# Spreading an output projection over all steps of an attention loop, with transposes a step later and other shares for three engines' copies

## Chip, core and metric

The kernel runs on one core of one Trainium2 chip. The metric is the device time of one execution in microseconds (us). Before the change the median of three runs is 1230.23 us (1226.86 to 1231.26).

## What is computed

Four layers are added to a residual stream `x` of 32 sequences, 32 tokens and 512 features, all in fp32. The first three mix features with weights picked per sequence. The fourth is attention with a paged cache, and the change is in it:

```python
q = einsum('bsd,ed->bse', x, Wq)   # 32 heads of 128
k = einsum('bsd,ed->bse', x, Wk)   # 8 heads of 128
v = einsum('bsd,ed->bse', x, Wv)
q = rope(rmsnorm(q, q_norm_w)); k = rope(rmsnorm(k, k_norm_w))
k_all = concat([k_cache[block_table], k])   # 512 cached keys and 32 new ones per sequence
v_all = concat([v_cache[block_table], v])
scores = where(valid, q @ k_all * SCALE, -1e30)
o = softmax(scores) @ v_all
x = x + o.reshape(b, s, 32 * 128) @ Wo.T
```

## The kernel before

**Two parts.** The first part (to about 421 us) does the three small layers and projects queries, keys and values. Queries, keys and new values go to DRAM scratch (`q_d`, `k_d`, `v_d`), and so does the residual stream (`x_d`). The second part is one loop of 264 steps (`for n in range(N + LAG)`), one step for each unit (sequence `b`, key head `g`): 32 sequences of 8 heads, and 8 steps to drain. A unit has four query heads times 32 tokens, so 128 rows. Four units of one sequence make a quad `(b, q)`, q = 0 or 1. Four sequences make a tile `t` of 128 tokens; there are 8 tiles.

**One step**, in the order in which it is written:

1. `scores` (lines 734, 735): two matmuls, 288 and 256 columns, into the one PSUM tile `s_ps`. VectorE then adds the mask and takes the row minimum in one pass (line 743), which frees `s_ps` for the next step.
2. `exponentials` (line 752): ScalarE, in place.
3. In steps 0, 2, 4 and 6 `projected(NCH - 1, FILLS[n], 2)`: the last piece of the value projection for one of four tiles that the first part left over (`FILL`, line 309).
4. From step 4 on, `place` for the quad that has been scored: step `n` handles part `j` of four of all four units at once. VectorE transposes 32x32 blocks into `turned` (line 765), and four copies of 32 partitions bring it into `placed`. ScalarE does `on_act` of the four (line 773), the rest goes to GpSimd when q = 0 (line 775) and to VectorE when q = 1 (line 777). `on_act` is 2, and 3 for q = 1 at the last part.
5. `share` (line 846, `f_ps`): the output projection of tile `t`, one or more of its 32 heads h, each one matmul of 512 columns, accumulated in one PSUM tile. The list `SHARE` says how many heads in which step; `BEGIN` is the first step, 36, and a tile has 32 steps. The list before has 30 entries, of which four are 0 and six are 2. The steps at 30 and 31 have none. So with n counted modulo 32, steps 2, 3, 17, 21, 25 and 29 project nothing. After the last head VectorE adds the residual (line 855) and SyncE stores the rows.
6. `values` (line 801, `o_ps`): four matmuls with the cached values for the unit of 8 steps ago. Its first matmul in a quad needs all four parts of `placed`. With the quad's last unit come the new values (line 813) and `keep`: VectorE takes the reciprocal of the sums (`rden`, line 825), scales `o_ps` into `os` (line 827) and transposes it into `ot` (line 830), which the output projection reads as weights. `ot` has three buffers, `os` and the residual tile `x3` one each.

**Loads.** At the first step of a sequence SyncE's queue issues, in this order: the second half of its queries (waits for the scores that used the buffer), its new values `vn` (wait for the matmuls of the sequence before the last), eight register loads with page numbers, the next sequence's new keys, its 16 pages of keys (line 194, 128 KB each), a page table; then, at the fifth step, the first half of the next sequence's queries (line 224). GpSimd issues four gathers of cached values (line 242). The instructions of PE, VectorE, ScalarE, GpSimd and SyncE stand in the loop's own order (`manual_schedule`); each engine works through its list in that order.

Of the kernel before, what the change touches and what calls it, by code (L numbers as in the profile page):

```python
# [12 lines left out]
F32 = mybir.dt.float32  # L13
I32 = mybir.dt.int32
AF = mybir.ActivationFunctionType
ALU = mybir.AluOpType
# [4 lines left out]
P = 128  # L21
# [36 lines left out]
def cond_resid_kernel(  # L58
# [104 lines left out]
    def load_table(b: int):  # L163

        pages_of[b] = const.tile([1, NPP], I32, tag="pages", name=f"pages_{b}", bufs=4)
        at = B + b * NPP
        nc.sync.dma_start(out=pages_of[b], in_=pick[:, at : at + NPP])

    class Picked:
# [18 lines left out]
                )  # L188
            )

        def transfer(self):
            for n, out in enumerate(self.dsts):
                row = self.src[ds(self.rows[n], 1)].rearrange(self.shape)
                self.eng.dma_start(out=out, in_=row)  # L194
                if len(self.rows) < len(self.dsts):
                    self.name_next()
# [24 lines left out]
    def load_queries(b: int, q: int):  # L221

        qts[b, q] = qp.tile([P, HALF * S], F32, tag="qt", name=f"qt_{b}_{q}")
        nc.sync.dma_start(
            out=qts[b, q], in_=q_d[b][:, q * HALF * S : (q + 1) * HALF * S]
        )
# [53 lines left out]
    def accumulator(name: str, long: bool = False):  # L280
        taken.append(name)
        pool = ps_m if long or len(taken) % 3 else ps_n
        return pool.tile([P, HID], F32, tag="mm", name=name)
# [17 lines left out]
        ws[c] = wqps[c % 2].tile([P, KC, HID], F32, tag="wq", name=f"wq_{c}")  # L301
        eng.dma_start(out=ws[c], in_=w_qkv[c])

    def project(c: int, t: int):
        w = ws[c]
        ps = accumulator(f"qkv_{c}_{t}", c >= (HQ + HK) // REP)
        x3 = x3t(t)
        for k in range(KC):
            nc.tensor.matmul(  # L309
                ps,  # L310
                x3[:, k, :],
                w[:, k, :],
                start=(k == 0),
                stop=(k == KC - 1),
            )
        if c >= (HQ + HK) // REP:
            c0 = (c - (HQ + HK) // REP) * HID
            vs = vsp.tile([P, HID], F32, tag="vs", name=f"vs_{c}_{t}")
            copied = nc.scalar.copy(vs, ps)
            if (c, t) == (NCH - 1, 0):  # L320

                with tc.issue_after(copied.ins):
                    nc.scalar.activation(warm, eps_t, AF.Exp)
            nc.scalar.dma_start(out=v_d[t * P : (t + 1) * P, c0 : c0 + HID], in_=vs)
            return None
        return SimpleNamespace(
            c=c, t=t, i=0 if c < HQ // REP else 1, ps=ps.rearrange("p (h d) -> p h d", h=REP)
        )
# [59 lines left out]
    def projected(c: int, t: int, lag: int):  # L388
        u = project(c, t)
        if u is not None:  # L390
            for stage in (squares, sums, roots, inverses, rotate, scales):
                stage(u)
            ready.append(u)
        if len(ready) > lag or (u is None and ready):
            store_heads(ready.pop(0))
# [364 lines left out]
    def place(b: int, q: int, j: int):  # L760
        if j == 0:
            placed[b, q] = tp.tile([P, QUAD, L // P, P], F32, tag="placed", name=f"placed_{b}_{q}")
        pr = prs[b, q][:, :, :L].rearrange("p u (c j s) -> p j u c s", j=P // S, s=S)[:, j]
        part = tp.tile([P, QUAD, L // P, S], F32, tag="turned", name=f"turned_{b}_{q}_{j}")
        nc.vector.transpose(part, pr)  # L765

        on_act = 3 if q == 1 and j == QUAD - 1 else 2
        for i in range(P // S):
            dst = placed[b, q][j * S : (j + 1) * S, :, :, i * S : (i + 1) * S]
            src = part[i * S : (i + 1) * S]  # L770
            dst, src = (a.rearrange("p u c s -> p (u c) s") for a in (dst, src))
            if i < on_act:
                nc.scalar.copy(dst, src)  # L773
            elif q == 0:
                nc.gpsimd.tensor_copy(dst, src)  # L775
            else:
                nc.vector.tensor_copy(dst, src)  # L777
# [14 lines left out]
    def values(b: int, g: int):  # L792
# [15 lines left out]
        if u == QUAD - 1:  # L808
# [5 lines left out]
            placed.pop((b, q)), prs.pop((b, q))  # L814
            keep(b, q)

    def keep(b: int, q: int):


        po = pos.pop((b, q))  # L820
        t, j = divmod(b, BT)
        if (t, q) not in ots:
            ots[t, q] = bp.tile([P, HALF, P], F32, tag="ot", name=f"ot_{t}_{q}")
        rden = tp.tile([P, QUAD], F32, tag="rden", name=f"rden_{b}_{q}")
        nc.vector.reciprocal(rden, dens.pop((b, q)))
        o = tp.tile([P, QUAD, D], F32, tag="os", name=f"os_{b}_{q}", bufs=1)
        nc.vector.tensor_tensor(  # L827
            o, po[:, :, :P], rden.unsqueeze(2).to_broadcast([P, QUAD, D]), ALU.mult
        )
        nc.vector.transpose(  # L830
            ots[t, q][:, :, j * S : (j + 1) * S],
            o.rearrange("p u (k d) -> p (u k) d", d=S),
        )

    pfs, x3s = {}, {}

    def load_residual(t: int):
        x3s[t] = tp.tile([P, HID], F32, tag="x3", name=f"x3_{t}", bufs=1)
        nc.sync.dma_start(out=x3s[t], in_=x_d[t])

    def finish(t: int, hs):

        for h in hs:
            if h == 0:
                pfs[t] = ps_p.tile([P, HID], F32, tag="f", name=f"f_ps_{t}")
            nc.tensor.matmul(  # L846
                pfs[t],
                ots[t, h // HALF][:, h % HALF, :],
                wo[:, h, :],
                start=(h == 0),  # L850
                stop=(h == HQ - 1),
            )
            if h == HQ - 1:
                x3 = x3s.pop(t)
                nc.vector.tensor_tensor(x3, x3, pfs.pop(t), ALU.add)
                nc.sync.dma_start(out=out[t * P : (t + 1) * P, :], in_=x3)

    LAG = 8

    SHARE = [1, 2, 1, 2] * 2 + [1, 2, 1] + [1, 1, 0, 1] * 4 + [1, 1, 2]
    BEGIN = BT * HK + LAG - QUAD

    def share(n: int):
        t, i = divmod(n - BEGIN, BT * HK)
        if 0 <= t < NT - 1 and i < len(SHARE):
            done = sum(SHARE[:i])
            finish(t, range(done, done + SHARE[i]))

    units = [(b, g) for b in range(B) for g in range(HK)]
    N = len(units)

    FILLS = {0: NT - 4, 2: NT - 3, 4: NT - 2, 6: NT - 1}
    order = {
        mybir.EngineType.PE,
        mybir.EngineType.DVE,
# [4 lines left out]
    with tc.manual_schedule(engines=order):  # L882
        for n in range(N + LAG):
            b, g = divmod(n, HK)
            if n == max(FILLS) + 1:
                pa.close()
                bp = ctx.enter_context(tc.tile_pool(name="b_w", bufs=3))
                ps_o = ctx.enter_context(tc.tile_pool(name="b_o", bufs=1, space=PSUM))
            if BEGIN <= n < N + QUAD and (n - BEGIN) % (BT * HK) == len(SHARE) - 2:

                load_residual((n - BEGIN) // (BT * HK))
            if n < N:
                if g == 0 and b >= 1:
                    load_queries(b, 1)
                    load_new_values(b)
                if g == 0 and 1 <= b < B - 1:
                    load_keys(b + 1)
                    keys = Picked(nc.sync, k_cache, pages_of.pop(b + 1), page_keys(b + 1), K_SHAPE)
                    load_new_keys(b + 1)
                    keys.transfer()  # L900
                    if b + 2 < B:
                        load_table(b + 2)
                if g == 0 and b >= 2:
                    load_values(b)
                if g == QUAD and b < B - 1:
                    load_queries(b + 1, 0)
                scored = scores(b, g)
                exponentials(*scored)
            if n in FILLS:

                projected(NCH - 1, FILLS[n], 2)
            if QUAD <= n < N + QUAD:
                bq, i = divmod(n - QUAD, HK)
                q, j = divmod(i, QUAD)
                if j == 0:
                    gather_new(bq, q)
                if j == 3:
                    flip_new(bq, q)
                place(bq, q, j)
            share(n)  # L920
            if n >= LAG:
                values(*units[n - LAG])
            if n < N and g == HK - 1 and b < B - 1:
                see_keys(b + 1)
            if n >= N + QUAD:
                at = 3 * (n - N - QUAD)
                finish(NT - 1, range(at, at + 3))
        assert not dens and not prs and not pos and not placed and not pns
        load_residual(NT - 1)
        finish(NT - 1, range(3 * QUAD, HQ))  # L930


# [74 lines left out]
```

## Time and profile before

| what | value |
|---|---|
| median of three runs | 1230.23 us |
| the profiled execution, its own time | 1226.37 us |
| its span, first to last instruction | 1224.6 us |
| granted TensorE clock | 0.999 |
| PE busy | 1183.7 us, 97% |
| VectorE (DVE) busy | 797.4 us, 65% |
| ScalarE (ACT) busy | 750.4 us, 61% |
| GpSimd (POOL) busy | 419.1 us, 34% |
| first scores of the loop start at | 421.55 us |
| scores of step 36 (first output projection) start at | 520.39 us |
| scores of step 132, 164 and 196 start at | 807.21, 902.82 and 998.78 us |
| scores of the last step with scores (255) start at | 1175.68 us |

A line of the timeline has the start in us, the duration in us, the engine, the kernel's line, the operation, what it writes and reads, and how many instructions are merged; in brackets stands the idle time before it and who ended it. A line of the waits has the waiting engine and line, the releaser, and then total us, times and the longest. One fp32 matmul of the kernel is two PE instructions, so "x2" is one matmul.

### The profile page before, as it was taken

The numbers are of one execution on the slowest core, as the hardware profiler recorded it, in microseconds if no ns is written. First come the engines' busy times: TensorE is split into PE (matmuls) and PEld (weight loads), VectorE is DVE, ScalarE is ACT, GpSimd is POOL, SyncE is SP. The second block draws the span as 40 slices with busy tenths as digits, with TensorE's granted clock in tenths as the row PEclk, the third lists the DMA queues.
The fourth block names the chain that finished last, engine by engine and source line by source line (L and its number), as shares of the span: only waits on it lengthen the run. The fifth ranks groups of instructions, "written<-read, shape, count | busy, mean of one in ns | idle before, by whom it ended". The sixth has DMA issues, their size and how long they took to land.

```text
span 1224.6 us, 19658 instructions
## 1 busy us (share of the span) xinstructions
PE 1183.7 (97%) x5480; PEld 749.1 (61%) x5480; DVE 797.4 (65%) x1787; ACT 750.4 (61%) x1657; POOL 419.1 (34%) x555
## 2 busy tenths in 40 slices
PE   8999999999999988899999999999999999999998
PEld 5444444444444456767767767767767777777764
DVE  3433597777774058866766777777767866876860
ACT  1233376565664268767767767867776776776760
POOL 2301443333332014434433433443334343433410
PEclk9999999999999999999999999999999999999999
DMA  8986756667655626766775676766666775776610
GB/s 323 420 333 254 261 144 153 168 178 198 160 124 161 213 84 219 234 217 194 226 228 188 219 230 201 229 199 220 220 210 196 243 224 173 247 227 188 215 57 9
DMA packets 180478, 250.63 MB, mean 205 GB/s; under 512 B 20978, under 2 KB 140146, under 8 KB 174610
## 3 DMA queue, kind: packets, MB, share of 16 engines
q1 hardware_dynamic: 157410, 165.35, 44.0%
q0 software_dynamic: 19216, 69.35, 16.7%
q10 hardware_dynamic: 3744, 14.68, 3.4%
q8 instruction: 44, 0.72, 0.2%
q14 instruction: 64, 0.52, 0.1%
HBM read 219.94 MB, written 29.36 MB: 204 GB/s over the span
## 4 chain that ended last, share of the span: by engine, by line
PE 82%; DVE 7%; DMA 3%; SPq 3%; issue 2%; ACT 1%; POOL 0%; ACTq 0%; DVEq 0%; POOLq 0%
PE qkv L309 27%; PE f_ps L846 17%; PE o_ps L801 15%; PE s_ps L734 10%; PE s_ps L735 7%; DMA wa<-in_w_adapt_dram 2%; PE adapt L530 2%; PE o_ps L813 2%; DVE pr L743 2%; DVE turned L765 2%; DVE placed L777 2%; PE base L510 1%; SPq L194 1%; DVE os L827 1%; DVE ot L830 1%
## 5 line engine op out<-in xcount | busy, mean ns | idle before, releaser
L773 ACT COPY placed<-turned 32x512 f32<-32x512 f32 x544 | 334.3, 615 | 9.2 <-DVE turned L765 2.7
L309 PE MATMUL qkv<-wq,x3t 128*128 128x512 f32 x768 | 332.1, 593 | 0.0
L801 PEld LDWEIGHTS o_ps<-vt,placed 128*128 128x128 f32 x2048 | 267.8, 192 | 105.1 <-issue 84.0
L752 ACT ACTIVATE pr<-pr,low 128x544 f32<-128x544 f32 x256 | 191.7, 749 | 194.6 <-DVE low L743 145.7
L743 DVE CUSTOM_DVE_ANT_0 pr<-s_ps,mask 128x544 f32<-128x544 f32 x256 | 184.3, 720 | 193.9 <-PE s_ps L735 151.8
L801 PE MATMUL o_ps<-vt,placed 128*128 128x128 f32 x2048 | 271.2, 276 | 10.2 <-ACT placed L773 7.6
L846 PE MATMUL f_ps<-wo,ot 128*128 128x512 f32 x512 | 251.1, 594 | 9.5 <-DVE ot L830 9.5
L309 PEld LDWEIGHTS qkv<-wq,x3t 128*128 128x128 f32 x768 | 145.3, 190 | 182.3 <-issue 182.1
L775 POOL COPY placed<-turned 32x512 f32<-32x512 f32 x256 | 155.8, 609 | 241.5 <-DVE turned L765 194.4
L734 PE MATMUL s_ps<-kt,qt 128*128 128x288 f32 x512 | 181.2, 436 | 11.4 <-DVE low L743 6.8
L765 DVE STREAM_TRANSPOSE turned<-pr 128x512 f32<-128x512 f32 x256 | 180.8, 706 | 0.1
L359 POOL TENSOR_TENSOR ra<-ra,rs 128x512 f32<-128x512 f32 x80 | 101.5, 1269 | 228.5 <-DVE rs L353 190.5
L735 PE MATMUL s_ps<-kt,qt 128*128 128x256 f32 x512 | 152.7, 380 | 0.0
L242 POOL DMA_INDIRECT vt<-in_v_cache_dram,v_idx x128 | 122.9, 960 | 53.5 <-issue 29.7
L363 ACT ACTIVATE ra<-ra,rinv 128x128 f32<-128x128 f32 x320 | 101.9, 390 | 45.8 <-DVE rinv L344 22.3
L846 PEld LDWEIGHTS f_ps<-wo,ot 128*128 128x128 f32 x512 | 92.4, 190 | 56.1 <-issue 33.5
L735 PEld LDWEIGHTS s_ps<-kt,qt 128*128 128x128 f32 x512 | 97.6, 191 | 27.0
L777 DVE COPY placed<-turned 32x512 f32<-32x512 f32 x224 | 96.1, 429 | 5.7
L734 PEld LDWEIGHTS s_ps<-kt,qt 128*128 128x128 f32 x512 | 77.5, 190 | 34.4 <-issue 11.8
L784 POOL COPY pq<-pr 128x128 f32<-128x128 f32 x64 | 18.9, 296 | 207.9 <-ACT pr L752 195.6
L827 DVE TENSOR_TENSOR os<-o_ps,rden 128x512 f32<-128x512 f32 x64 | 44.3, 692 | 57.7 <-PE o_ps L813 56.4
L332 ACT ACTIVATE sq<-qkv 128x512 f32<-128x512 f32 x80 | 47.0, 588 | 50.4 <-PE qkv L309 49.5
(90 smaller groups left out, 740.7 us busy)
## 6 DMA issues: line engine op xcount, KB each, us to landing
kt<-in_k_cache_dram SPq DMA_DIRECT2D x512, 128.0 KB
wa<-in_w_adapt_dram SPq DMA_DIRECT2D x32, 1024.0 KB
q_d<-st SPq DMA_DIRECT2D x256, 64.0 KB
qt<-q_d SPq DMA_DIRECT2D x64, 256.0 KB
wq<-in_w_qkv_dram ACTq DMA_DIRECT2D x10, 1024.0 KB
wo<-in_w_o_dram SPq DMA_DIRECT2D x16, 512.0 KB
k_d<-st SPq DMA_DIRECT2D x64, 64.0 KB
v_d<-vs ACTq DMA_DIRECT2D x16, 256.0 KB
```

The costliest lines, as they stand in the source:

```text
L242: nc.gpsimd.indirect_dma_start(out=vts[b][:, c, :], out_offset=None, in_=v_cache, in_offset=bass.IndirectOffsetOnAxis(ap=v_idx[:, at : at ...
L309: nc.tensor.matmul(ps, x3[:, k, :], w[:, k, :], start=(k == 0), stop=(k == KC - 1),)
L734: nc.tensor.matmul(ps[:, first:L], q, kt4[:, :N_LOW, g, :], start=True, stop=True)
L735: nc.tensor.matmul(ps[:, L : first + LT], q, kt4[:, N_LOW:, g, :], start=True, stop=True)
L743: nc.vector.tensor_tensor_reduce(pr, ps[:, first : first + LT], mask, -SCALE, 3.0e38, ALU.add, ALU.min, low)
L752: nc.scalar.activation(pr, pr, AF.Exp, bias=low, scale=-1.0, accum_out=dens[quad][:, u : u + 1])
L765: nc.vector.transpose(part, pr)
L773: nc.scalar.copy(dst, src)
L775: nc.gpsimd.tensor_copy(dst, src)
L777: nc.vector.tensor_copy(dst, src)
L801: nc.tensor.matmul(po[:, u, :P], pt[:, c, :], vt[:, c, g * D : (g + 1) * D], start=(c == 0), stop=False,)
L846: nc.tensor.matmul(pfs[t], ots[t, h // HALF][:, h % HALF, :], wo[:, h, :], start=(h == 0), stop=(h == HQ - 1),)
```

## The change

It has five parts.

- **Output projection.** `SHARE` is now one head in every step but two steps with 2, no zeros; `BEGIN` is 37. Modulo 32, only steps 3 and 4 project nothing. The tile's store is issued from ScalarE's queue in the step after its last head instead of from SyncE's; the residual is loaded in the same step as before (modulo 32, step 0), while its add moves from step 1 to step 2.
- **Transposes of outputs.** `keep` stops after `os`; the transpose into `ot` is done at the head of the next step (`flip_kept`), after that step's scores pass on VectorE. For the second quad of a tile's first sequence it waits until step 18 modulo 32. `os` has two buffers, which the residual tile now shares.
- **Last values.** The projection of the four left-over tiles is cut in halves: two matmuls in each of steps 0 to 7 instead of four in each of steps 0, 2, 4 and 6.
- **Copies.** For the first four sequences alone: `on_act` is 1, 2, 1, 2 over the four parts where GpSimd takes the rest (q = 0, and both quads of sequence 0), and 3, 2, 3, 2 where VectorE takes it.
- **Loads.** 12 of the 16 key pages stay at a sequence's first step; the first queries of the next sequence and then the last 4 pages and the page table come at the fifth.

```diff
-        for k in range(KC):
+        for k in range(KC) if half is None else range(half * KC // 2, (half + 1) * KC // 2):
...
-        on_act = 3 if q == 1 and j == QUAD - 1 else 2
+        on_pool = q == 0 or b == 0
+        if b >= BT:
+            on_act = 3 if q == 1 and j == QUAD - 1 else 2
+        elif on_pool:
+            on_act = 1 + j % 2
+        else:
+            on_act = 3 - j % 2
...
-            elif q == 0:
+            elif on_pool:
                 nc.gpsimd.tensor_copy(dst, src)
...
-        o = tp.tile([P, QUAD, D], F32, tag="os", name=f"os_{b}_{q}", bufs=1)
+        o = tp.tile([P, QUAD * D], F32, tag="os", name=f"os_{b}_{q}")
...
-        nc.vector.transpose(
-            ots[t, q][:, :, j * S : (j + 1) * S],
-            o.rearrange("p u (k d) -> p (u k) d", d=S),
-        )
+        at = BT * HK * (b // BT) + LAG + HK + QUAD - 2 if (b % BT, q) == (0, 1) else 0
+        kept.append((b, q, o, at))
+
+    def flip_kept(n: int):
+        while kept and kept[0][3] <= n:
+            b, q, o, _ = kept.pop(0)
+            t, j = divmod(b, BT)
+            if (t, q) not in ots:
+                ots[t, q] = bp.tile([P, HALF, P], F32, tag="ot", name=f"ot_{t}_{q}")
+            nc.vector.transpose(
+                ots[t, q][:, :, j * S : (j + 1) * S],
+                o.rearrange("p (k d) -> p k d", d=S),
+            )
...
-        x3s[t] = tp.tile([P, HID], F32, tag="x3", name=f"x3_{t}", bufs=1)
+        x3s[t] = tp.tile([P, HID], F32, tag="os", name=f"x3_{t}")
...
-    SHARE = [1, 2, 1, 2] * 2 + [1, 2, 1] + [1, 1, 0, 1] * 4 + [1, 1, 2]
-    BEGIN = BT * HK + LAG - QUAD
+    SHARE = [1, 1, 2, 1, 1, 1, 1, 1, 2, 1, 1, 1, 1, 1] + [1] * HALF
+    BEGIN = BT * HK + LAG - QUAD + 1
...
+        elif 0 <= t < NT - 1 and i == len(SHARE):
+            store_sum(t, nc.scalar)
...
-                    keys.transfer()
-                    if b + 2 < B:
-                        load_table(b + 2)
+                    keys.transfer(slice(0, 12))
...
                 if g == QUAD and b < B - 1:
                     load_queries(b + 1, 0)
+                    if b >= 1:
+                        keys.transfer(slice(12, NPP))
+                    if 1 <= b < B - 2:
+                        load_table(b + 2)
...
-            if n in FILLS:
-                projected(NCH - 1, FILLS[n], 2)
+            flip_kept(n)
+            if n - n % 2 in FILLS:
+                project(NCH - 1, FILLS[n - n % 2], half=n % 2)
```

More of the change, by code (lines that the diff above doesn't have):

```diff
@@ L189, in name_next, with transfer @@
             )
-        def transfer(self):
-            for n, out in enumerate(self.dsts):
+        def transfer(self, part):
+            for n, out in list(enumerate(self.dsts))[part]:
                 row = self.src[ds(self.rows[n], 1)].rearrange(self.shape)
@@ L302, in load_qkv, with project @@
         eng.dma_start(out=ws[c], in_=w_qkv[c])
-    def project(c: int, t: int):
+    halves = []
+    def project(c: int, t: int, half=None):
         w = ws[c]
-        ps = accumulator(f"qkv_{c}_{t}", c >= (HQ + HK) // REP)
+        ps = halves.pop() if half == 1 else accumulator(f"qkv_{c}_{t}", c >= (HQ + HK) // REP)
         x3 = x3t(t)
-        for k in range(KC):
+        for k in range(KC) if half is None else range(half * KC // 2, (half + 1) * KC // 2):
             nc.tensor.matmul(
@@ L315, in project @@
             )
+        if half == 0:
+            halves.append(ps)
+            return None
         if c >= (HQ + HK) // REP:
@@ L815, in values @@
             keep(b, q)
+    kept = []
     def keep(b: int, q: int):
         po = pos.pop((b, q))
-        t, j = divmod(b, BT)
-        if (t, q) not in ots:
-            ots[t, q] = bp.tile([P, HALF, P], F32, tag="ot", name=f"ot_{t}_{q}")
         rden = tp.tile([P, QUAD], F32, tag="rden", name=f"rden_{b}_{q}")
         nc.vector.reciprocal(rden, dens.pop((b, q)))
-        o = tp.tile([P, QUAD, D], F32, tag="os", name=f"os_{b}_{q}", bufs=1)
+        o = tp.tile([P, QUAD * D], F32, tag="os", name=f"os_{b}_{q}")
         nc.vector.tensor_tensor(
-            o, po[:, :, :P], rden.unsqueeze(2).to_broadcast([P, QUAD, D]), ALU.mult
-        )
-        nc.vector.transpose(
-            ots[t, q][:, :, j * S : (j + 1) * S],
-            o.rearrange("p u (k d) -> p (u k) d", d=S),
-        )
-    pfs, x3s = {}, {}
+            o.rearrange("p (u d) -> p u d", d=D),
+            po[:, :, :P],
+            rden.unsqueeze(2).to_broadcast([P, QUAD, D]),
+            ALU.mult,
+        )
+        at = BT * HK * (b // BT) + LAG + HK + QUAD - 2 if (b % BT, q) == (0, 1) else 0
[10 more added lines that the diff above has]
+            )
+    pfs, x3s, added = {}, {}, {}
     def load_residual(t: int):
-        x3s[t] = tp.tile([P, HID], F32, tag="x3", name=f"x3_{t}", bufs=1)
+        x3s[t] = tp.tile([P, HID], F32, tag="os", name=f"x3_{t}")
         nc.sync.dma_start(out=x3s[t], in_=x_d[t])
@@ L855, in finish, with store_sum @@
                 nc.vector.tensor_tensor(x3, x3, pfs.pop(t), ALU.add)
-                nc.sync.dma_start(out=out[t * P : (t + 1) * P, :], in_=x3)
+                added[t] = x3
+    def store_sum(t: int, eng):
+        eng.dma_start(out=out[t * P : (t + 1) * P, :], in_=added.pop(t))
     LAG = 8
-    SHARE = [1, 2, 1, 2] * 2 + [1, 2, 1] + [1, 1, 0, 1] * 4 + [1, 1, 2]
-    BEGIN = BT * HK + LAG - QUAD
+    SHARE = [1, 1, 2, 1, 1, 1, 1, 1, 2, 1, 1, 1, 1, 1] + [1] * HALF
+    BEGIN = BT * HK + LAG - QUAD + 1
     def share(n: int):
@@ L869, in share @@
             finish(t, range(done, done + SHARE[i]))
+        elif 0 <= t < NT - 1 and i == len(SHARE):
+            store_sum(t, nc.scalar)
     units = [(b, g) for b in range(B) for g in range(HK)]
     N = len(units)
-    FILLS = {0: NT - 4, 2: NT - 3, 4: NT - 2, 6: NT - 1}
+    FILLS = {2 * i: NT - FILL + i for i in range(FILL)}
     order = {
@@ L884, in cond_resid_kernel @@
             b, g = divmod(n, HK)
-            if n == max(FILLS) + 1:
+            if n == max(FILLS) + 2:
                 pa.close()
@@ L888, in cond_resid_kernel @@
                 ps_o = ctx.enter_context(tc.tile_pool(name="b_o", bufs=1, space=PSUM))
-            if BEGIN <= n < N + QUAD and (n - BEGIN) % (BT * HK) == len(SHARE) - 2:
+            if BEGIN <= n < N + QUAD and (n - BEGIN) % (BT * HK) == len(SHARE) - 3:
                 load_residual((n - BEGIN) // (BT * HK))
@@ L929, in cond_resid_kernel @@
         load_residual(NT - 1)
+        flip_kept(N + LAG)
         finish(NT - 1, range(3 * QUAD, HQ))
+        store_sum(NT - 1, nc.sync)
 def _laid_out(i):
```

## Prediction

> **What bounds the kernel now.** I read the page first, then PE's waits, then PE's timeline unit by unit, and beside its gaps the timelines of ScalarE, VectorE and SyncE's queue.
>
> ```profile
> PE 1183.7 (97%) x5480; PEld 749.1 (61%) x5480; DVE 797.4 (65%) x1787; ACT 750.4 (61%) x1657; POOL 419.1 (34%) x555
> ```
>
> PE looks full, so the question is how much of the 97% is matmul at its rate. One score matmul pair starts 0.92 us before the next matmul (0.49 + 0.43), the four value matmuls 0.89, one head of the output projection 0.86. In a step with one head the next scores start 2.67 us later, with two 3.53, without any at best 1.81; a step that ends a quad adds 0.64 (new values and a transpose), and the step after it 0.10. For 32 steps with 32 heads and 8 quads: 32x1.81 + 32x0.86 + 8x0.74 = 91.3 us. The trace has 95.6 (scores of steps 132 and 164 start at 807.21 and 902.82). So 4.3 us per tile are PE waiting, and that is all that a better order can win there.
>
> Waits of PE (total, times, longest):
>
> ```profile
> PE f_ps L846 <- DVE ot L830: 9.5, 7, 1.4
> PE o_ps L801 <- ACT placed L773: 7.6, 5, 2.4
> PE s_ps L734 <- DVE low L743: 6.8, 18, 0.8
> ```
>
> Seven times, once per tile, the first head waits for `ot`. PE's timeline there (steps 163, 164, 165):
>
> ```profile
> 900.27 0.75 PE L734 MATMUL s_ps<-kt,qt 128*128 128x288 f32 x2
> ...
> 902.82 0.75 PE L734 MATMUL s_ps<-kt,qt 128*128 128x288 f32 x2
> 903.41 0.59 PE L735 MATMUL s_ps<-kt,qt 128*128 128x256 f32 x2
> 905.36 1.12 PE L846 MATMUL f_ps<-wo,ot 128*128 128x512 f32 x2 [1.36 <-DVE ot L830]
> ...
> 907.21 0.65 PE L734 MATMUL s_ps<-kt,qt 128*128 128x288 f32 x2
> ```
>
> This step (4 modulo 32) takes 4.39 us where 2.77 of work stand. ScalarE at the same time:
>
> ```profile
> 902.52 0.75 ACT L752 ACTIVATE pr<-pr,low 128x544 f32<-128x544 f32 x1 [0.18 <-DVE low L743]
> ...
> 903.27 0.24 ACT L790 COPY pn<-pn_ps 128x128 f32<-128x128 f32 x1
> 903.53 1.87 ACT L773 COPY placed<-turned 32x512 f32<-32x512 f32 x3
> ```
>
> Its three copies end at 905.40, as late as the wait that PE names (`ot` ends at 905.30), and the next value matmuls need them. The reader is to see two waits one behind the other, of which PE names only the first. Step 20, which has no output projection, shows the second bare:
>
> ```profile
> 478.59 0.59 PE L735 MATMUL s_ps<-kt,qt 128*128 128x256 f32 x2
> 480.63 1.16 PE L801 MATMUL o_ps<-vt,placed 128*128 128x128 f32 x8 [1.44 <-ACT placed L773]
> ```
>
> The rest of the 4.3 us, from the starts of successive scores: steps 17 and 25 have no head and take 2.37 instead of 1.81 (VectorE is late with the mask pass), 1.1 together; the steps after the quads of second halves (0, 8, 16, 24) lose 0.12 to 0.15 because the transpose and the mask stand ahead of the pass, 0.6; and some ten steps lose one bubble of 0.1, 1.0. With 1.6 for step 4 that is 4.3.
>
> In the first 36 steps (421.55 to 520.39, 98.8 us) the work is 77 us. Eight steps with the left-over values:
>
> ```profile
> 427.81 0.75 PE L734 MATMUL s_ps<-kt,qt 128*128 128x288 f32 x2 [0.83 <-DVE low L743]
> ```
>
> A step with scores alone can't be shorter than scores, mask pass, scores: 1.91 us, of which PE works 0.92. Later SyncE's queue limits:
>
> ```profile
> 473.76 11.31 SPq L194 DMA_DIRECT2D kt<-in_k_cache_dram  x16
> 485.17 0.30 SPq L167 DMA_DIRECT2D pages<-in_pick_dram  x1
> 485.57 1.51 SPq L224 DMA_DIRECT2D qt<-q_d  x2
> ```
>
> ```profile
> 490.04 0.72 PE L734 MATMUL s_ps<-kt,qt 128*128 128x288 f32 x2 [1.88 <-DMA qt<-q_d]
> ```
>
> Step 24's queries are issued behind 16 pages and arrive 4.2 us later.
>
> [...] 97% busy, yet 4.3 of 95.6 us per tile are waits, partly inside the modelled ends. [...] Here an issue is 0.33 us on SyncE's and on ScalarE's queue, so the moved store is worth no more.
>
> **The change, part by part.** Sums are against the profiled execution, 1226.4 us; the median of the runs, 1230.2, lies 3.9 above it.
>
> *Heads in every step.* The 0.1 bubbles, steps 17 and 25 and the late pass after quads all sit where scores wait for VectorE. With one head in the step PE has 2.67 us, and the pass must be done 1.91 after the scores' start, so VectorE may be 0.7 late for nothing. Checked in the busiest stretch, steps 0 to 3: VectorE per step is pass to transpose 0.65, to copies 0.74, two copies 0.89, so 2.28; step 0 adds the transpose into `ot` 0.71 and starts 1.45 after the scores (`os` and the mask stand ahead); step 2 adds the residual 0.72. Starts of scores: 0, 2.77, 5.44, 8.11. VectorE is through with step 0 at 1.45+2.28+0.71 = 4.44, with 1 at 6.72, with 2 at 9.72. Step 3's pass could start at 9.23 and starts at 9.72: 0.5 late, less than 0.7. None of these losses stays: 4.3 - 1.6 = 2.7 us per tile gone. Not all: the bound from the other side is a bubble of 0.1 in six of these steps.
>
> *A step later.* Step 4 has no head now, so the wait for `ot` goes; the first head, step 5, needs `ot` well after it is made. What is late next is the copies. Continuing: step 3's row minimum is ready at 9.72+0.73 = 10.45, the exponential starts 0.04 later, and from its start to the third copy's end it takes 905.40-902.52 = 2.88: 13.37. Step 4's scores start at 8.11+2.45 = 10.56 and are through at 11.58; the value matmuls start at 13.43, wait 1.85, and the step takes 3.74. Its work is 1.91. Before, without its head, it took 4.39-0.86 = 3.53. So this part wins nothing; it costs 0.2 per tile. The wait has two ends: 1.2 if VectorE isn't late, 2.6 if the residual and `ot` both fall ahead of the pass. I take 1.85.
>
> Per tile: 2.7 - 0.2 = 2.5, less 0.1 for a remaining bubble: 2.4. Six whole tiles lie between step 36 and 228: 14.4. Steps 228 to 255 lack steps 0 to 3: 1.9. Sum 16.3.
>
> *Transposes a step on.* 64 of 0.711 us as before; hidden behind the heads, worth their 0.7 only where a step has none (counted in step 4). `os` in two buffers lets the next one be written; the residual tile lies in the same two from step 0 to the store at step 3, and the quad that wants its buffer comes at step 7: no wait. The transpose at step 18 follows the head of that step in PE's list, 0.2 us at most, under a slack of 0.7.
>
> *Store on ScalarE's queue.* 0.33 in step 3, behind the copies and ahead of step 4's exponential, which isn't needed for four steps: nothing. SyncE's list loses 0.33 per tile.
>
> *Halves.* Every one of steps 0 to 7 has 0.92 + 4x0.43 = 2.64 of PE work, over 1.91: four waits of 0.99+0.1 go. 4.1 us to step 8, with the transpose of step 7 counted. ScalarE's copies of values (0.58 and 0.33 to issue) fall into odd steps; each fits in 2.64 on average.
>
> *Shares.* Sequence 0: VectorE's 7 copies of 0.43 go to GpSimd, whose 20 copies of 0.61 fill 12.2 of 20 us. Sequences 1 to 3: ScalarE 16 copies instead of 17, VectorE 6 for 7, GpSimd 10 for 8. ScalarE then needs, in the four steps of a second half, 4x0.85 + 0.25 + 10x0.615 = 9.8 us and binds there, where before it was 9.2 and VectorE bound. At the quad's end two copies instead of three save 0.6 of the wait in steps 12, 20, 28. By step 16 I count 6 us in all. From step 15 to 24 SyncE's chain binds (25.0 us, of which 22.6 would be enough for the engines); the pages now come last instead of the queries, the bytes ahead are the same, so the chain only starts earlier, with step 15: still 6. Steps 24 to 36 add 0.5. At the beginning: 6.5, between 4 and 10.
>
> *Loads in later steps.* Between steps 23 and 32 of a tile SyncE's chain takes up to 25.5 us, the engines 26.1: hidden, with 0.6 to spare; other sequences have over 1.
>
> *Sum.* 16.3 + 6.5 = 22.8: 1226.4 becomes 1203.6, and the median 1230.2 becomes 1207.4; I say 1207. The drain from step 256 holds the same work and the same wait of 2.45 for copies: nothing.
>
> **Rivals.**
>
> *The copies aren't late.* If step 4's wait falls to about 0.4, another 1.4x7 = 10 us go: 1197. For it: ScalarE has idle time in steps 0 to 2. Against: its list puts the exponential ahead of the copies, and step 20 shows 1.44 without any head near it. Chance 0.18.
>
> *VectorE becomes the bound in second halves.* Four such steps hold 9.8 to 10.5 us of VectorE against 10.6 to 10.8 of PE. If each window loses 0.4 (four per tile, 7 tiles) 11 us are given back: 1218. For it: the margin at steps 26 and 2 is only 0.2. Against: steps 18 and 26 show no wait after their scores now. Chance 0.13.
>
> *Slower: the last four pages are late.* They stand behind queries that wait for PE, and no step may start without its sequence's keys. Today's chain lands 25.5 us after the scores of the last step of the sequence before, against 26.1 (one sequence in four) and some 27. If it grows by 3 us, 7 sequences wait 2.4 and 21 wait about 1.5: 48 us, less 23: 1255. It decides from about 2.1 us on, where 7x(2.1-0.6) + 21x(2.1-1.5) is 23. Against: the slot of those queries is free after the fourth scores, 11 us after the chain starts, and SyncE reaches them only after 16. Chance 0.07.
>
> **Chances.** The forecast 0.62, with its own range 1200 to 1214. A difference of about 0.5% (6 us) is what a measurement of this kernel can tell from none. Faster by more: 0.62 + 0.18 + 0.11 of the second rival = 0.91, taken as 0.90; within: 0.04; slower: 0.06. The range must reach to both faster rivals: 1196 to 1218.
>
> **What would show it.** Right: scores of steps 132 and 164 some 93.2 us apart; no wait of `f_ps` for `ot`, but seven waits of `o_ps` for ScalarE's `placed` of about 1.7 us, in steps 4 modulo 32; steps 17 and 25 at 2.67 with a head; step 36 starting near 514. Wrong: scores waiting for `kt` or `qt` in steps divisible by 8 after step 36; scores waiting for `low` in steps 1, 2, 9, 17, 25; or step 4 under 2.5 us.

## The result, and the profile after

The kernel after takes 1207.74 us (median of four runs, 1205.86 to 1208.37) against 1229.19 for the kernel before (four runs, 1226.86 to 1231.26): a ratio of 0.982, 95% interval 0.980 to 0.985. The forecast was 1207. The sum behind it holds in the steady loop and is too large at both ends: 22.8 us forecast, 18.4 measured between the profiled executions, 21.5 between the medians. That the median was met within 1 us is partly luck: the profiled execution before (1226.37) lies 2.8 below its median, the one after at its median.

The profiled execution took 1207.95 us (span 1206.1, clock 0.996), 18.4 less than the profiled one before. From the starts of scores:

| stretch | before | after | difference | predicted |
|---|---|---|---|---|
| up to step 0 (same code) | 421.55 | 420.50 | -1.05 | 0 |
| steps 0 to 8 | 25.34 | 21.18 | -4.16 | -4.1 |
| steps 8 to 36 | 73.50 | 72.25 | -1.25 | -2.4 |
| steps 36 to 68 | 95.61 | 95.28 | -0.33 | -2.4 |
| steps 68 to 228, five tiles | 478.38 | 466.59 | -11.79 | -12.0 |
| steps 228 to 255 | 81.30 | 79.47 | -1.83 | -1.9 |
| drain | 48.9 | 50.9 | +2.0 | 0 |

The page's line of busy time has hardly moved: PE is 11.7 us less busy and still at 97%.

```profile
PE 1172.0 (97%) x5480; PEld 745.0 (62%) x5480; DVE 790.9 (66%) x1777; ACT 753.1 (62%) x1649; POOL 432.9 (36%) x573
```

The waits of PE after the change (total us, times, longest). The wait of `f_ps` for `ot` is gone from the list; the one for ScalarE's copies has grown from 7.6 to 17.5.

```profile
PE o_ps L813 <- ACT placed L785: 17.5, 11, 2.4
PE s_ps L739 <- DVE low L748: 3.4, 5, 1.4
...
PE s_ps L740 <- DMA vn<-v_d: 1.6, 1, 1.6
```

PE's timeline at steps 164 and 165 (line 739 and 740 are the two score matmuls, 813 the cached values), and ScalarE beside it:

```profile
889.22 0.75 PE L739 MATMUL s_ps<-kt,qt 128*128 128x288 f32 x2
889.81 0.59 PE L740 MATMUL s_ps<-kt,qt 128*128 128x256 f32 x2
892.01 1.16 PE L813 MATMUL o_ps<-vt,placed 128*128 128x128 f32 x8 [1.60 <-ACT placed L785]
```

```profile
889.08 0.75 ACT L757 ACTIVATE pr<-pr,low 128x544 f32<-128x544 f32 x1 [0.77 <-DVE low L748]
...
890.09 1.87 ACT L785 COPY placed<-turned 32x512 f32<-32x512 f32 x3
```

Step 4 modulo 32 takes 3.78 us (next scores at 893.00). From the exponential's start to the third copy's end are 890.09 + 1.87 - 889.08 = 2.88 us, the figure that the prediction used, and the values start 0.05 after that. Against a start at PE's rate (0.43 after 889.81) that is a wait of 1.77; the line shows 1.60 because it counts from the modelled end. The stall has stayed (1.62 over the step's work before, 1.87 now); only its named releaser changed. All other steps of a tile run at PE's rate: 2.67 with one head, 3.53 with two, 3.31 at a quad's end (4.17 with two heads, 2.45 in step 3, without one), 2.77 after it (step 20 loses another 0.15). Steps 132 to 164 take 93.33 us, before 95.61.

What went the other way is PE's clock. The windows view gives, for stretches of the drain, their length and each engine's busy time and instructions (PE, its weight loads, DVE, ACT, POOL); the last three figures are the granted clock, DMA's share and GB/s. First the time up to the long wait of the drain, then the 3.41 us that begin 1.1 us after it.

```profile
1155.00:1165.70 10.70, 10.70 (x74) 7.79 (x73) 8.21 (x18) 7.78 (x16) 2.74 (x5) 1.00 0.01 2
1169.32:1172.73 3.41, 3.41 (x6) 1.33 (x5) 0.00 (x0) 0.00 (x0) 0.00 (x0) 0.50 0.33 79
```

PE waits 2.45 us for copies in the drain, before and after. After the wait the clock is 0.50 for 3.41 us in this execution (a half-clock window, from here on); it was not in the one before. Half of 3.41 is 1.7 us of PE work (the three heads after the wait take 4.44 us here and 2.74 before): most of the +2.0. A second such window began at 517.37, after a wait of 1.90 in step 36, and took most of the first tile's gain: steps 36 to 68 take 93.5 in runs 2 and 9, which have no window there. The profile before has one too, at 491.34 in steps 24 and 25, which the prediction does not mention.

### The profile page after: what moved, and what is told of

It is laid out like the page before. It is cut to its first block, busy times and chain, and to the rows that moved or that the text cites. A ratio compares the mean times of both kernels' runs of the same rounds, so it can differ in the third digit from the quotient of the medians.

```text
span 1206.1 us, 19664 instructions
## 1 busy us (share of the span) xinstructions
PE 1172.0 (97%) x5480; PEld 745.0 (62%) x5480; DVE 790.9 (66%) x1777; ACT 753.1 (62%) x1649; POOL 432.9 (36%) x573
## 4 chain that ended last, share of the span: by engine, by line
PE 87%; DVE 7%; ACT 3%; issue 2%; DMA 1%; POOL 1%; another core or an unknown queue 0%; ACTq 0%; DVEq 0%; POOLq 0%
PE qkv L311 27%; PE f_ps L871 17%; PE o_ps L813 16%; PE s_ps L739 9%; PE s_ps L740 8%; PE adapt L535 2%; PE base L515 2%; PE o_ps L825 2%; DVE turned L770 2%; ACT placed L785 2%; DVE pr L748 2%; DVE placed L789 1%; ACT pr L757 1%; PE base L516 1%; DVE ot L855 0%
## 5 line engine op out<-in xcount | busy, mean ns | idle before, releaser
L813 PE MATMUL o_ps<-vt,placed 128*128 128x128 f32 x2048 | 272.6, 276 | 19.9 <-ACT placed L785 17.5
L871 PE MATMUL f_ps<-wo,ot 128*128 128x512 f32 x512 | 256.8, 597 | 0.0
L787 POOL COPY placed<-turned 32x512 f32<-32x512 f32 x274 | 167.4, 611 | 225.8 <-DVE turned L770 179.9
L739 PE MATMUL s_ps<-kt,qt 128*128 128x288 f32 x512 | 174.9, 423 | 3.4 <-DVE low L748 3.4
L789 DVE COPY placed<-turned 32x512 f32<-32x512 f32 x214 | 93.2, 436 | 5.5
```

The lines of the kernel that those rows point to most:

```text
L739: nc.tensor.matmul(ps[:, first:L], q, kt4[:, :N_LOW, g, :], start=True, stop=True)
L813: nc.tensor.matmul(po[:, u, :P], pt[:, c, :], vt[:, c, g * D : (g + 1) * D], start=(c == 0), stop=False,)
L871: nc.tensor.matmul(pfs[t], ots[t, h // HALF][:, h % HALF, :], wo[:, h, :], start=(h == 0), stop=(h == HQ - 1),)
```

## The experiments

The theory: heads in every step hide VectorE's lateness (16 us); the halves are worth 4; step 4 waits for ScalarE's third copy; shares and loads are worth little. The rivals are in the expectations. "Tile" is 32 steps, from step 68 on. Ratios are to the kernel before, beside which each was run.

**1. The heads alone.** The kernel after with the rest of its change put back but for what the heads need (the store on ScalarE's queue, `os` in two buffers, one transpose per tile kept back until step 18): the edits of runs 2, 3 and 4 below, and

```diff
         kept.append((b, q, o, at))
+        if not at:
+            flip_kept(0)
```

> The kernel before with the new SHARE and BEGIN alone (and what they need: the store a step later, the transpose of each tile's fifth-step buffer kept back until step 18). Transposes again at the end of their own step, left-over values whole in steps 0, 2, 4, 6, the old shares of copies, all 16 pages first. Theory (heads in every step hide the waits for VectorE): scores of steps 132 and 164 some 93.3 us apart, as in the kernel after (95.6 before), steps 0 to 36 as before (98.8), so about 16 us less than before, 1213. Rival (the transposes a step later are what makes room): VectorE starts its pass 0.7 us late after every quad, scores wait for it in steps 1, 9, 17 and 25, tiles stay at 94.5 or more and the time is 1219 or more. Step 4: the theory says its wait is 1.7 and for the copies, if the transposes stay in their step too.

Measured: 1217.61 us (1215.1 to 1220.16), ratio 0.991 (0.989 to 0.994). A tile takes 93.82, between both expectations. PE's timeline at steps 24, 25 and 26 of a tile:

```profile
866.27 0.75 PE L739 MATMUL s_ps<-kt,qt 128*128 128x288 f32 x2
...
869.19 0.75 PE L739 MATMUL s_ps<-kt,qt 128*128 128x288 f32 x2
...
871.96 0.65 PE L739 MATMUL s_ps<-kt,qt 128*128 128x288 f32 x2
```

The two steps take 2.92 and 2.77 us; the kernel after has 2.77 and 2.67. So with a head in the step and the transpose still ahead of the pass, the scores two steps on come 0.25 late, after steps 8, 24 and 0 of a tile (not after 16, whose transpose is kept back): 0.7 us. In step 4 the wait is 0.2 shorter (1.55 for 1.77). So of the 2.3 us per tile the heads give 1.8 and the transposes a step later 0.5. The total lies 4.6 above the expected 1213: seven tiles of 0.5 are 3.5, and the rest is within the scatter of the runs (this profile has three half-clock windows from step 0 on).

**2. Whole projections again.**

```diff
-            if n - n % 2 in FILLS:
-                project(NCH - 1, FILLS[n - n % 2], half=n % 2)
+            if n in FILLS:
+                projected(NCH - 1, FILLS[n], 2)
```

> The kernel after, with the left-over value projections whole in steps 0, 2, 4 and 6 again. Theory (the halves fill four steps that were pure waiting): steps 0 to 8 take 25.3 us again instead of 21.2, the rest as in after, 4.1 us more: about 1212. Rival (SyncE's chain of loads sets when step 24 or 32 starts in any case, so that the 4 us are given back): the start of step 36 moves by less than 1.5 us, about 1208.5.

Measured: 1208.05 us (1207.43 to 1211.74), ratio 0.985 (0.982 to 0.988). Steps 0 to 8 take 25.33 again, yet step 36 comes only 1.4 us later after step 0 than in the kernel after (94.86 for 93.43). The 4.2 us are real and most of them are given back before step 36, as the rival has it, though loads account for only part of it (step 32, run 4): see runs 9 to 11 for the rest.

**3. Old shares of copies.**

```diff
-        on_pool = q == 0 or b == 0
-        if b >= BT:
-            on_act = 3 if q == 1 and j == QUAD - 1 else 2
-        elif on_pool:
-            on_act = 1 + j % 2
-        else:
-            on_act = 3 - j % 2
+        on_pool = q == 0
+        on_act = 3 if q == 1 and j == QUAD - 1 else 2
```

> The kernel after, with the copies of the first four sequences shared as before. Theory (they win what the quads' ends lost, some 2 us between steps 8 and 24): step 36 starts 1 to 2 us later, about 1209; the rest is the same. Rival 1 (loads bind in steps 15 to 32): no difference, below 0.5 us. Rival 2 (the waits of 1.8 us at steps 8 and 20 that the kernel after still has are made by the new shares): step 36 starts earlier, by up to 2 us.

Measured: 1208.15 us (1205.49 to 1209.38), ratio 0.984 (0.981 to 0.986). Steps 0 to 36 take 94.66 for 93.43, of which 1.7 are a half-clock window. The old shares lose 1.1 in steps 8 to 16, and from there to 36 they are 1.6 ahead without that window: this profile has no late start of VectorE (see run 9), the one of the kernel after has two. So neither the theory nor rival 2 is borne out: net of the window the new shares win nothing (they cost 0.5), and step 8, whose wait rival 2 laid to them, takes 3.68 with both. Rival 1's number fits; its reason, the loads, isn't tested by this run.

**4. All pages first.**

```diff
-                    keys.transfer(slice(0, 12))
+                    keys.transfer(slice(0, NPP))
+                    if b < B - 2:
+                        load_table(b + 2)
...
-                    if b >= 1:
-                        keys.transfer(slice(12, NPP))
-                    if 1 <= b < B - 2:
-                        load_table(b + 2)
```

> The kernel after, with all 16 key pages and the page table at a sequence's first step again, ahead of the first queries of the next sequence. Theory (the order matters only where the loads bind, and the bytes ahead are the same): step 24 waits about 1.9 us for its queries again, step 32 no longer waits 1.7 us for its last pages; step 36 within 1 us of the kernel after, later steps unchanged: 1207 to 1209. Rival (the pages in two pieces are worth something in the steady tiles, since queries then arrive earlier): tiles of 32 steps grow from 93.3 us by 0.5 or more, 1211 or more.

Measured: 1205.62 us (1204.62 to 1206.27), ratio 0.982 (0.980 to 0.984). Steps 16 and 24 wait 0.6 and 1.6 us for queries again, step 32 for nothing, and step 36 comes 1.65 us earlier than in the kernel after. Tiles stay at 93.31 except one with a half-clock window (94.98). So pages in two pieces win nothing. In the profile of the kernel after step 32 waits between its two score matmuls; the timeline:

```profile
502.81 0.75 PE L739 MATMUL s_ps<-kt,qt 128*128 128x288 f32 x2
505.19 0.67 PE L740 MATMUL s_ps<-kt,qt 128*128 128x256 f32 x2 [1.63 <-DMA vn<-v_d]
```

The second score matmul reads the later pages. SyncE had issued the last four at 498.69 to 500.57; the releaser that is named belongs to the same queue. When the pages landed isn't shown; that they are what is late is inferred. For it speaks run 6, whose step 32 waits 1.1 us at the same matmul and names the pages. In run 5, the same kernel, step 32 starts 3.0 us after the last of these issues instead of 2.2 and doesn't wait. So the mechanism of the slower rival comes once in an execution or not at all, not 28 times.

This drain has no half-clock window: the same stretch as above has 16 PE instructions for 6, and the drain takes 49.2 us, not 50.9. The wait of 2.45 ends at 1168.19 in both profiles and the same work follows, so the clock alone makes the difference.

```profile
1169.32:1172.73 3.41, 3.41 (x16) 1.98 (x15) 0.00 (x0) 0.00 (x0) 0.00 (x0) 1.00 0.28 79
```

**5. The kernel after once more**, beside runs 6 to 8.

> The kernel after, unchanged, beside the next three. It tells what of the first 36 steps belongs to the kernel and what to one execution. If the 1.3 and 1.6 us that steps 18 and 26 lost to late signals and the half-clock windows are chance, steps 16 to 24 take 19.6 us and 24 to 32 19.9; if they come with the kernel, 21.0 and 20.7 again. Tiles 93.3 apart, time 1207.7 within 2.

Measured: 1207.74 us (1205.82 to 1209.68), ratio 0.984 (0.982 to 0.986). Tiles 93.3. The late starts are there again, in steps 18, 26 and now 34 (0.6, 0.9 and 1.0 us late), so they come with the kernel. The half-clock windows lie elsewhere (step 20 and the drain), so those are chance in their place.

**6. Two copies on ScalarE instead of three, at the last quad of a tile.**

```diff
-            on_act = 3 if q == 1 and j == QUAD - 1 else 2
+            on_act = 3 if q == 1 and j == QUAD - 1 and b % BT < BT - 1 else 2
```

> The kernel after, with ScalarE doing two copies instead of three at the last part of the last quad of every tile; VectorE does the other two. Theory (step 4 of a tile waits for ScalarE's third copy alone, and VectorE has room for one more): the wait there falls from 1.75 to 1.15 us, tiles of 32 steps take 92.7 instead of 93.3, about 4 us less in all: 1203.5. Rival (VectorE, which is late in step 3, ends its own copies as late): the wait is 1.6 or more and names VectorE, time unchanged within 1 us.

Measured: 1202.41 us (1201.91 to 1203.51), ratio 0.980 (0.978 to 0.982). Tiles take 92.97: the wait falls by 0.32, not the 0.6 expected. PE's waits name a new releaser:

```profile
PE o_ps L813 <- DVE os L837: 10.2, 7, 2.5
PE o_ps L813 <- ACT placed L785: 5.7, 5, 1.7
```

The values of a new quad also need `o_ps` free, so VectorE's scaling of the quad before (`os`, which the extra copy pushes back by 0.43) is next in line: it ends 2.32 us after the start of the scores, ScalarE's last copy at 2.10 and the third copy, before, at 2.74. The theory held for the first 0.3. The medians differ by 5.3 us from run 5, the profiles by 4.1: 2.1 in steps 68 to 255 (six of some 0.35), 1.6 in the drain, which has no half-clock window here, 0.4 before step 68. All five executions have a granted clock of 0.998 to 1.000, those of run 5 0.996 or 0.997; whether that is the edit's doing or chance isn't shown.

**7. One head in each of the 32 steps.**

```diff
-    SHARE = [1, 1, 2, 1, 1, 1, 1, 1, 2, 1, 1, 1, 1, 1] + [1] * HALF
+    SHARE = [1] * HQ
...
-        at = BT * HK * (b // BT) + LAG + HK + QUAD - 2 if (b % BT, q) == (0, 1) else 0
+        at = BT * HK * (b // BT) + LAG + HK + QUAD + 1 if (b % BT, q) == (0, 1) else 0
...
-        if 0 <= t < NT - 1 and i < len(SHARE):
-            done = sum(SHARE[:i])
-            finish(t, range(done, done + SHARE[i]))
-        elif 0 <= t < NT - 1 and i == len(SHARE):
-            store_sum(t, nc.scalar)
+        if i == 0 and t >= 1:
+            store_sum(t - 1, nc.scalar)
+        if 0 <= t < NT - 1:
+            finish(t, range(i, i + 1))
...
-                place(bq, q, j)
+                if n % (BT * HK) != QUAD:
+                    place(bq, q, j)
             share(n)
+            if QUAD <= n < N + QUAD and n % (BT * HK) == QUAD:
+                place(bq, q, j)
```

> The kernel after, with exactly one head of the output projection in each of the 32 steps of a tile, so that steps 3 and 4 have one too and no step has two; the residual is added in step 4 ahead of that step's transpose. Theory (step 4's wait is a step too short by the 1.7 us that two heads would fill; the copies need their time whatever PE does): the wait falls to 0.2 or less, tiles take 91.5 us instead of 93.3, six of them and part of the drain: about 1196. Rival 1 (copies follow PE's pace, the wait moves along): the wait stays above 1 us, tiles at 92.5 or more, 1203 or more. Rival 2 (the one PSUM buffer of the projection): the first head of the next tile in step 5 waits for the add, 0.5 to 0.9 us each.

Measured: 1190.40 us (1189.79 to 1191.41), ratio 0.970 (0.968 to 0.972). Tiles take 91.31. PE at steps 163 to 165:

```profile
876.32 0.65 PE L739 MATMUL s_ps<-kt,qt 128*128 128x288 f32 x2
...
879.63 0.75 PE L739 MATMUL s_ps<-kt,qt 128*128 128x288 f32 x2
...
880.65 1.02 PE L871 MATMUL f_ps<-wo,ot 128*128 128x512 f32 x2
881.51 1.05 PE L813 MATMUL o_ps<-vt,placed 128*128 128x128 f32 x8
882.40 0.65 PE L739 MATMUL s_ps<-kt,qt 128*128 128x288 f32 x2
```

Step 4 takes 2.77 with its head: no wait at all, nor does step 5 wait for the PSUM buffer; both rivals fall. The third copy ends 1.45 us after the start of step 4's scores instead of 2.74: 0.86 is the head of step 3, the other 0.43 goes with the residual's add, which the edit also moves (in the kernel after it stood ahead of step 3's mask pass, at 887.72). The head of step 4 covers another 0.86. The two heads alone make 1.72 of the 1.77; they were not run without the other moves. The 17 us against run 5 are, in the profiles: five tiles of 2.0 (step 4, and the 0.15 of step 20); 1.0 in steps 36 to 68 (step 36 has no head and still waits); 2.9 in steps 228 to 255, which two heads leave for the drain; 2.0 in the drain (48.9 for 50.9), where the heads cover the wait of 2.45 and no half-clock window follows; 1.1 before step 36, where run 5 has such a window and this profile has none.

**8. The same with all pages first.**

> As the one before, with all 16 key pages first as well. Theory (orders of loads matter only in the first 36 steps, where pages first took 1.7 us less in one profile): the tiles as in the kernel before this one, steps 0 to 36 within 2 us of it, the time the same within 2 us, 1195. Rival (with less time per tile the loads bind, and two pieces are then better): scores wait for queries in steps divisible by 8, 1198 or more.

Measured: 1190.23 us (1190.03 to 1190.97), ratio 0.970 (0.968 to 0.972). Tiles 91.31: no difference. In the steady tiles the order of these loads is worth nothing at either pace, and here it is worth nothing in the total.

**9. New keys at the fifth step.** The timeline of the kernel after at step 18 (VectorE and SyncE's queue):

```profile
466.32 0.85 DVE L789 COPY placed<-turned 32x512 f32<-32x512 f32 x2
...
466.93 0.06 SPq L219 DMA_DIRECT2D kt<-k_d  x1
...
468.43 0.72 DVE L748 CUSTOM_DVE_ANT_0 pr<-s_ps,mask 128x544 f32<-128x544 f32 x1 [1.26 <-remote]
```

VectorE is idle for 1.26 us and starts 1.91 after the last instruction of the scores that it waits for (466.52); elsewhere in this profile an idle VectorE mostly starts 0.42 to 0.53 after that. The load of the new keys shows an issue of 0.06 instead of 0.34, and SyncE's next one comes 1.4 us later. The edit moves that load behind the 12 pages:

```diff
-                    load_new_keys(b + 1)
                     keys.transfer(slice(0, 12))
...
                     if b >= 1:
+                        load_new_keys(b + 1)
                         keys.transfer(slice(12, NPP))
```

> The kernel after, with the next sequence's new keys loaded at a sequence's fifth step instead of its first, behind the 12 pages and ahead of the queries and last pages. In the kernel after, VectorE's pass starts 0.7 to 1.4 us late in two or three of steps 18, 26 and 34, with idle VectorE, and each time SyncE issues that one load within 0.6 us of the scores while GpSimd issues gathers. Theory (the issue of that load at that moment is what delays the signal): the late starts go, steps 16 to 24 and 24 to 32 take 19.6 and 19.9 us, step 36 starts 2 to 3 us earlier, 1205. Rival (the delay belongs to GpSimd's gathers, or to the length of the step): step 18 or 26 is late again, and the time is 1207 or more.

Measured: 1205.27 us (1204.71 to 1208.42), ratio 0.983 (0.980 to 0.986). Steps 0 to 36 take 90.74 for 93.43. The timeline at step 18:

```profile
468.63 0.85 DVE L789 COPY placed<-turned 32x512 f32<-32x512 f32 x2
469.51 0.72 DVE L748 CUSTOM_DVE_ANT_0 pr<-s_ps,mask 128x544 f32<-128x544 f32 x1
```

No idle time is left, nor in steps 26 and 34. In the profile the theory holds and the rival falls; the median is within the scatter of run 5.

**10. Both.** Run 7 with this edit.

> One head in each of the 32 steps, as in the run at 1190.4, with the new keys loaded at the fifth step. Theory: as in the run before this, 2 to 3 us less up to step 36, the tiles at 91.3: 1188. Rival: no difference, 1190.4.

Measured: 1190.36 us (1188.61 to 1193.27), ratio 0.971 (0.968 to 0.974). In the profile steps 0 to 36 take 91.18 for run 7's 93.05, with no late start, but the median is the same. Not shown to be faster.

**11. Run 7 with whole projections.**

> One head in each of the 32 steps, as in the run at 1190.4, with the left-over value projections whole in steps 0, 2, 4, 6 again. The first 8 steps are then 4.16 us longer. If the halves are worth what they save there, 1194.5. If most of it is given back before step 36 (late signals in steps 18 and 26 and late pages in step 32, which the kernel with whole projections after the change did not have), step 36 moves by 1 to 2 us: 1191.5 to 1192.

Measured: 1196.25 us (1192.65 to 1197.33), ratio 0.976 (0.973 to 0.978). The profiled execution is the fastest of the four; in it steps 0 to 36 take 94.94, 1.9 more than run 7 and 3.8 more than run 10, which has no late starts either. So the halves keep 3.8 of their 4.2 us where the new keys are out of the way (runs 2 and 9 say the same: 94.86 and 90.74), and 1.4 to 1.9 where they aren't. The medians say 5.9 here and 0.3 in run 2: they don't size it.

**12. Run 7 with the old shares.**

> One head in each of the 32 steps, as in the run at 1190.4, with the copies of the first four sequences shared as before. With the heads out of the way the difference is that of the shares alone. My prediction had them at 2 us up to step 24; in the first test of this edit steps 8 to 24 took 42.65 us, of which 1.7 were a half-clock window, against 40.4 in the kernel after. So 0.5 to 1.5 us: 1191.4. Rival: the new shares bring VectorE's and PE's pattern into the late signals, so that the old ones are as good: 1190.4.

Measured: 1190.24 us (1189.62 to 1192.91), ratio 0.971 (0.968 to 0.974). Steps 0 to 36: 92.96 against 93.05 in run 7, without any late start. In the profiles the rival holds: what the new shares win in steps 8 to 16 (1.1) the late starts take back. Against run 10, which has the new shares and no late start, the old ones cost 1.8.

## Why the prediction was right, point by point

**Heads in every step.** The size, 2.4 us per tile, was right (2.36), its division was not. The prediction gave 2.7 to the heads and called the transposes a step later "worth their 0.7 only where a step has none". Run 1 shows 1.8 and 0.5. Its own numbers held the answer: a pass that begins 1.45 after the scores begins at 1.45 + 0.71 = 2.16 if the transpose is still ahead of it (868.40, or 2.13, in run 1). The next scores start 0.79 after the pass begins (869.19), so at 2.95 by these numbers, where PE's own work would let them start at 2.77. In run 1 they start at 2.92, and the step after it loses another 0.10: the 0.25.

**Step 4.** Right in the releaser, in the wait (1.85 forecast, 1.77 measured) and in the step (3.74; 3.72 to 3.79). That the wait isn't a property of the copies but of too few heads in steps 3 and 4 was not seen; run 7 shows it, and it is worth 2 us per tile.

**Halves.** 4.1 forecast to step 8, 4.16 measured. **The beginning as a whole** fell short: 6.5 forecast to step 36, 5.4 measured, and some 0.8 of that is the half-clock window of the profile before (its steps 24 to 28 take 10.07, those of run 1, in the same order and without it, 9.26). The failing step is "Steps 24 to 36 add 0.5". By step 24 the gain was 6.9 for "still 6", and SyncE's chain, said to bind there, made step 24 wait for nothing; the 12 steps from there took 31.86 for 30.35. Late starts in steps 18 and 26 (1.2 and 0.9) and the wait in step 32 (1.1) took 3.2 in all. With the new keys moved (run 9) 2.7 of it come back. "Step 36 near 514" came true (513.93) by luck: the first part, the same code, was 1.05 faster.

**Shares.** Forecast at 1.9 by step 16 (the 6 less the 4.1 of the halves); 1.1 in steps 8 to 16 and nothing net (runs 3 and 12), since the late starts came with them. Beside a kernel without late starts the old shares cost 1.8 (run 12 against run 10).

**Loads in later steps: hidden.** Right: no scores wait for keys or queries after step 36.

**Drain: nothing.** Wrong by 2.0. The work and the wait of 2.45 are the same; the clock after the wait is not. In the profile after it was 0.50 for 3.41 us, from 1.13 us after the end of the wait on; in those before and of run 4 it was 1.00 after the same wait. In the loop, windows of 3.41 us began 1.30 us after the end of a wait of 1.88 (step 24 of the profile before, from 491.34) and 0.36 after that of 1.90 (step 36 of the one after); none followed the ten other idle times of PE of over 1.4 us (1.43 to 1.66) in the loop of the profile after. What decides it is not shown: the length of the wait alone does not, since 2.45 went both ways.

**Rivals.** "The copies aren't late" needed a wait of 0.4: it was 1.77. VectorE's bound in second halves doesn't show: steps 26 and 2 take 2.67. The late pages came in step 32 alone, and not in run 5.

**What stays open.** Why VectorE's pass starts late (1.91 us after the last score instruction begins in step 18, mostly 0.42) where one load is issued beside the scores: the late starts of steps 18, 26 and 34 all stand beside a short issue record and go with it, but a short record 0.24 us before step 34 of the first profile (508.87), and others later in the loop, stand beside no late start. That it is PE's signal which is late is inferred from VectorE's idle time. Run 11 has no short record and no late start with the load in its old place, so the moment counts and not the place in the list. Also open is the size of the halves in the medians.

## What to carry to other kernels

A stall whose named releaser is removed may only change its name: look for what else ends at the same moment, and count what would cover it. If an engine that works in order has filler work, spread it so that no step is without it, those first that wait for another engine's long chain: the two heads that this change had doubled elsewhere, put into the two steps that it left empty, took off another 17 us, of which some 3 are half-clock windows that the slower kernel's profile has and the faster one's hasn't. When several edits are made together, a right sum doesn't show that its terms are right; undoing all but one does.

## What was not expected of the hardware

From the loop's start on, 3.41 us at a granted clock of 0.50 followed waits of PE of 1.88 us (before), 1.90 and 2.45 us (after), up to 1.7 us lost each time; the same wait of 2.45 had none after it in the profiles before and of run 4. In run 1 such windows came three times between the loop's start and the end. It is part of the scatter between executions: the profiles of one and the same kernel after (the first and run 5) have them in different places. An idle VectorE, which mostly starts 0.42 us after the last score instruction begins, started 1.91 and 1.61 us after it in steps 18 and 26 of the kernel after, and 1.32 us after it in step 18 of run 5.
